# A layer kernel's value product: eight full products against seven products of halves, woven into the next unit's mixing

## The chip, the core and the metric

The kernel runs on one core of one Trainium2 chip. A core has a matrix engine (TensorE: PE for its products, PEld for its weight loads), a vector engine (VectorE: DVE), an activation engine (ScalarE: ACT), a general engine (GpSimd: POOL) and a queue that issues most transfers (SyncE: SP). Each engine takes its own instructions in the order in which the program emitted them and waits where an operand is not there yet. The metric is the device time of one execution in microseconds (us); the median of three runs of the kernel before is 1118.88 us (1118.39 to 1120.43).

## What is computed

One layer for x of 4 batches, 2048 tokens, 512 channels, all in f32: a linear recurrence, and after it the part that the change touches, a channel mix with a shift by one token:

```python
x_prev = concat([zeros, x[:, :-1]])              # x is the normalized, modulated h
xr = mu_r * x + (1 - mu_r) * x_prev
xk = mu_k * x + (1 - mu_k) * x_prev
r = sigmoid(xr @ W_r.T)                          # receptance
k_act = square(relu(xk @ W_k.T))                 # key
out = r * (k_act @ W_v.T)                        # value
...
x = x + gb * out                                 # gb: a gate per batch and channel
```

## The kernel before

The work is cut into 32 units of 256 tokens. Unit i is stretch i // 4 of batch i % 4; `at` below is i % 4. Two chains of units run at once, eight units apart: `Finish` (a unit's residual, normalization, key, receptance and value) and `Gates` (the projection for the recurrence of unit i + 8). The scan of the recurrence is a list of small DVE jobs handed out between by `take_share`, with the shares of a unit in SHARES. The order on every engine is the order of the calls, written out by hand.

A unit i from the fifth on does this on PE: the two "direct" products and the state products of unit i + 1 (L538, L493), woven between the seven products of the key (`seven`, L663, 28 matmuls of 128 columns, two PE instructions each); the seven products of the receptance (14 matmuls of 256 columns) with half of the projection of unit i + 8 (L244) between; then `mix` of unit i + 1, which begins with eight transposes (L600); the rest of the projection; and the value product (L760, eight matmuls of 512 columns). Units 0 to 3, 25 and 26 make the receptance with full products (L745), and units 0 to 3 the key too (L633).

`seven` makes seven products p1, p7, p6, p4, p5, p2, p3 in three PSUM tiles x, y, z. p1, p6, p5 and p3 use x one after the other and accumulate in it, p7 and p4 use z. After p1, p7, p6 and p3 ACT copies the tile out (L672, L675, L678, L690: the copies of the quarters c00, c11, c10, c01); after p4, p5 and p2 DVE adds it (L681, L684, L687). So p6 can't start before the copy of c00 is done, nor p4 before that of c11, p5 before that of c10, p3 before p5's addition. `emit` puts other jobs behind each product. Before `seven`, DVE makes four sums of quarters of the operand that varies (`sums_t` for the key, L779 to L782; `sums_s` for the receptance, L772 to L775).

`mix` of unit i + 1 (L585): after the transposes, eight times a pair of ACT (L606) and DVE (L609), the first four for the key, then POOL's edge column (L612), the four key sums and a small POOL copy behind them (L617), then `between` (both sigmoids of unit i on ACT, L737, and POOL's shift of the residual x of unit i + 2, L463), then four pairs for the receptance, a second edge and two small copies of the carry (L620). After it come, on DVE, `multiply` (L252: g, the projection times the row bc that came by DMA), on ACT `deliver` (L267: four instructions), the norm of a later unit's raw rows (L186, L192), and then the value product with its evictions on DVE (L763 times r, L764 plus x) and the store (L766).

The value weights carry the gate gb, so there is one set for each batch: the first four units scale w_v by gb (L978), turn it by 16 transposes (L992), copy it out (L996) and keep it in DRAM; a later unit fetches its set back, 1 MB a unit (L806). `Turn` does the same for D, scaled by ga, and that stays.

Of the kernel before, what the change touches and what calls it, by code (L numbers as in the profile page):

```python
# [21 lines left out]
P = 128  # L22
B, T, D, M = 4, 2048, 512, 64
KC = D // P
W = 256
# [22 lines left out]
def adaln_layer_kernel(ctx: ExitStack, tc: tile.TileContext, x, x_t, c_t, wmod, w_gate, w_b, b_gate, b_f, c_mat, d_mat,  # L48
# [18 lines left out]
    gb = const.tile([P, KC, B], F32, name="gb")  # L67
    d0 = const.tile([P, B, D], F32, name="d0")
# [6 lines left out]
    wvb = const.tile([P, B, KC, D], F32, name="wvb")  # L75
# [17 lines left out]
    d0c = const.tile([P, KC, B], F32, name="d0c")  # L93
# [344 lines left out]
    class Finish:  # L438
# [13 lines left out]
        def load(self):  # L452
            u = self.u
            if not hasattr(self, "x"):
                self.room()
                load_natural(u, self.x)
            if not hasattr(self, "h"):
                self.h = room_transposed(u)
                load_transposed(u, self.h)

        def shift(self, engine=nc.gpsimd):
            xt = self.x
            engine.tensor_tensor(xt, xt, d0[:, self.u.b, :].unsqueeze(1).broadcast_to([P, NT, D]), ALU.add)  # L463
# [121 lines left out]
        def mix(self, between):  # L585
            xn, b = self.xn, self.u.b
            mixed = self.mixed = p1.tile([P, 2, KC, W], F32, tag="mixed", name=f"mixed_{self.tag}")
            edge = p2.tile([P, 2, KC], F32, tag="edge", name=f"edge_{self.tag}")
# [6 lines left out]
            pts = []  # L595
            for g in range(KC // 2):
                pt = ps2.tile([P, 2, W], F32, tag="pt", name=f"pt_{self.tag}_{g}")
                for j in range(2):
                    for n in range(NT):
                        nc.tensor.transpose(pt[:, j, ts(n, P)], xn[:, n, ts(2 * g + j, P)], ident)  # L600
                pts.append(pt)

            for i in (1, 0):
                for k in (0, 2, 1, 3):
                    pt, m = pts[k // 2][:, k % 2, :], mixed[:, i, k, :]
                    nc.scalar.activation(  # L606
                        m, pt, AF.Identity, bias=mod[:, SB, k, b : b + 1], scale=now_f[:, b, i, k : k + 1]
                    )
                    nc.vector.scalar_tensor_tensor(  # L609
                        m[:, 1:], pt[:, : W - 1], prev_f[:, b, i, k : k + 1], m[:, 1:], ALU.mult, ALU.add  # L610
                    )
                nc.gpsimd.tensor_tensor(mixed[:, i, :, 0], mixed[:, i, :, 0], edge[:, i, :], ALU.add)  # L612
                if i == 1:
                    if self.fast:
                        self.key_sums()

                        nc.gpsimd.tensor_copy(edge[:, 1, 0:1], self.sums[:, 3, 1, W // 2 - 1 :])  # L617
                    between()
            for g, pt in enumerate(pts):
                nc.vector.tensor_copy(carry[:, b, 2 * g : 2 * g + 2], pt[:, :, W - 1])  # L620
# [88 lines left out]
        def key_sums(self):  # L709
            self.sums = self.half_of(dg[:, 3])  # L710
            sums_t(self.sums, self.token_quarters(1))
# [12 lines left out]
        def receptance_sums(self):  # L724
            self.r_sums = self.half_of(wvb[:, 3])
            sums_s(self.r_sums, list(zip(*self.token_quarters(0))))
# [8 lines left out]
        def sigmoids(self):  # L735
            for r in self.r:
                nc.scalar.activation(r, r, AF.Sigmoid)  # L737
# [12 lines left out]
        def value(self, between, parts=1):  # L750

            act, xt, u = self.act, self.x, self.u
            n_col = D // parts
            for n in range(NT):
                r = self.r[n]
                for h in range(parts):
                    at = ts(h, n_col)
                    pv = ps2.tile([P, D], F32, tag="pm", name=f"pv_{self.tag}_{n}_{h}")[:, :n_col]
                    for j, k in enumerate(range(KC) if parts == 1 else (2, 3, 0, 1)):
                        nc.tensor.matmul(  # L760
                            pv, act[:, k, ts(n, P)], wvb[:, self.at, k, at], start=(j == 0), stop=(j == KC - 1)
                        )
                    nc.vector.tensor_mul(r[:, at], pv, r[:, at])  # L763
                    nc.vector.tensor_add(r[:, at], r[:, at], xt[:, n, at])  # L764
                    queue = nc.scalar if h else nc.sync
                    queue.dma_start(out[u.b, u.t0 + n * P : u.t0 + (n + 1) * P, at], r[:, at])  # L766
                if n == 0:
                    between()
# [8 lines left out]
    def sums_t(t, b):  # L777
        (b00, b01), (b10, b11) = b
        nc.vector.tensor_sub(t[:, 0], b01, b00)  # L779
        nc.vector.tensor_sub(t[:, 1], b11, t[:, 0])  # L780
        nc.vector.tensor_sub(t[:, 2], b11, b01)
        nc.vector.tensor_sub(t[:, 3], b10, t[:, 1])  # L782

    def quarters_of(w, output_first=False):
# [4 lines left out]
    key_weights, receptance_weights = (  # L789
        room.rearrange("p k d -> p (k d)").rearrange("p (i k o) -> p i k o", i=4, k=2) for room in (dg[:, 2], wvb[:, 2])  # L790
    )

    kept = {
        name: [dram.tile([P, KC * D], F32, tag=f"{name}{b}", name=f"{name}{b}") for b in range(B)]
        for name in ("dg", "wv")
    }

    def keep_in_dram(name, b):
        src = dg if name == "dg" else wvb
        nc.sync.dma_start(kept[name][b], src[:, b].rearrange("p k d -> p (k d)"))  # L800

    def fetch(name, i):

        if 6 <= i < len(fin):
            dst = dg if name == "dg" else wvb
            nc.sync.dma_start(dst[:, i % 2].rearrange("p k d -> p (k d)"), kept[name][i % B])  # L806
# [56 lines left out]
    dn, wn = wr, wvb[:, 3]  # L863
    room = p2.tile([P, B, W], F32, tag="y", name="room").rearrange("p b w -> p (b w)")
    cn = room[:, :D].rearrange("p (k n) -> p k n", k=KC)
    d0row = room[:B, D:]

    ct, sig = d0c, off
# [156 lines left out]
    def shift_rows():  # L1025

        t = dram.tile([B, D], F32, tag="d0", name="d0_rows")
        nc.sync.dma_start(t, d0row)
        nc.sync.dma_start(d0, t.unsqueeze(0).broadcast_to([P, B, D]))
# [60 lines left out]
    weights_to(wn, w_v, nc.sync)  # L1090
# [16 lines left out]
    turn_v = [Turn(wvb[:, b], wn, gb, b, None, "v") for b in range(B)]  # L1107
# [17 lines left out]
    for e in range(KC):  # L1125
        nc.tensor.transpose(pr[:B, ts(e, P)], d0c[:, e, :], ident)
    nc.scalar.copy(d0row, pr[:B, :])
# [3 lines left out]
    keep_in_dram("dg", 0)  # L1131
# [17 lines left out]
    keep_in_dram("dg", 1)  # L1149
# [17 lines left out]
    turn_v[0].rows()  # L1167
# [40 lines left out]

    EIGHT = (25,26)
    SHARES = ((0,0,2,1.7,4.4, 0, 1.8), (5.4, 0.0, 1.8, 1.8, 3.6, 0.0, 1.8), (0.3, 0, 0.1, 0.1, 0.2, 0.03, 0.1))  # L1210
    for i, f in enumerate(fin):
        at = i % B
        ahead = fin[i + 1] if i + 1 < len(fin) else None
        if i < 4:
            if i == 3:
                take(100)
            fin[i + 2].load()
            gts[i + 10].load()
            f.key()
            if i == 0:  # L1220
# [22 lines left out]
            turn(turn_v[i])  # L1243
            keep_in_dram("wv", i)
            if i == 3:
                fetch("dg", i + 3)
# [13 lines left out]
            ahead.mix(fin[i + 2].shift)  # L1260
# [6 lines left out]
            if i < 3:  # L1267
                turn_v[i + 1].rows()
            f.value(lambda: take(3 if i == 0 else 4))
            if i < 2:  # L1270
                turn(turn_d[i + 2], turn_c[i + 2])
                keep_in_dram("dg", i + 2)
                gates(8 if i == 0 else 10)
        else:


            held = at == B - 2 and i > 4
# [6 lines left out]
            if not late:  # L1284
                load_finish()
            shares = [0] * 7
# [23 lines left out]
            def first_norm(j):  # L1310
                if j < len(gts):
                    gts[j].norm()

            def transfers(j):

                if j < len(gts):
                    gts[j].send()
                if j + 1 < len(gts):
                    gts[j + 1].load()
                fetch("wv", j - 7)  # L1320

            def spread():
                if 4 < i < len(gts) - 8:
                    gts[i + 8].spread()
# [5 lines left out]
            if not ahead:  # L1330
# [10 lines left out]
                f.squares(0)  # L1341
                f.emit(other[5:])
                finish = None
            elif late:
# [5 lines left out]
                f.emit(f.key_fast(), {1: [filler(d, 1), lambda: first_norm(i + 8)], 7: [filler(d, 1)],  # L1350
                                      6: [filler(d, 1)], 4: [filler(d, 1), f.receptance_sums],
                                      5: [filler(d, 1)], 2: [filler(d, 1)]})
                if i > 4:
                    transfers(i + 8)
                spread()
                fetch("dg", i + 3)
# [7 lines left out]
                          6: [filler(gate, 1), finish_norm], 4: [filler(gate, 1), lambda: f.squares(1)]}  # L1364
            else:
# [6 lines left out]
                                      6: [filler(d, 2), scans[1], acts[1], stats(0)],  # L1372
                                      4: [filler(d, 2), scans[2]], 5: [filler(d, 1), scans[3]],
                                      2: [stats(1, 0)], 3: [stats(1, 1), scans[4]]})
                fetch("dg", i + 3)
                spread()
# [3 lines left out]
                          5: [lambda: f.squares(1)]}  # L1380
# [5 lines left out]
            elif ahead:  # L1386
                f.emit(f.receptance_fast(), finish)

            def between():
                if not eight:  # L1390
                    f.sigmoids()
# [3 lines left out]
            if ahead:  # L1395
                ahead.mix(between)
            else:
                f.sigmoids()
            if i + 9 < len(gts):
                gts[i + 9].load_t()  # L1400
            fill(gate, len(gate))
# [3 lines left out]
            if not held:  # L1405
                first_norm(i + 9)
            f.value(scans[6], parts=1 if ahead else 2)
            if not held:
                transfers(i + 9)
# [46 lines left out]
```

## Time and profile before

| what | us |
|---|---|
| median of three runs | 1118.88 |
| span of the profiled execution | 1117.2 |
| PE busy | 1092.6 |
| DVE busy | 777.3 |
| ACT busy | 666.1 |
| POOL busy | 188.7 |
| one steady unit (value start to value start) | 32.1 |

PE is busy for all but about 25 us of the span, and these lie at the start and at the very end. The other engines are busy for two thirds of it or less. Matmuls overlap their neighbours in the records, so the time that one takes is read from start to start. A projection ("pg"), a direct product ("pd"), a key, receptance or value product ("px", "py", "pz" with the letter k or r, and "pv") can be told by the names of the tiles that they write.

### The profile page before, as it was taken

To read this page: it belongs to the slowest core of one execution; us is meant where nothing else is said; L and a number is where in the kernel's file an instruction comes from. 1 tells how busy PE (TensorE), PEld (TensorE's weight loads), DVE (VectorE), ACT (ScalarE), POOL (GpSimd) and SP (SyncE) were. 2 spreads that over 40 slices of the span, in tenths; PEclk is the share of its full clock that TensorE was granted. 3 is DMA by queue.
4 is the path that set the end of the run, shared out by engine and by line. 5 is a ranking of instruction groups with operands and counts; after the bars stand their busy time and mean duration, and the time that the engine had idled before them with its cause. 6 is when DMAs were issued, how large, how long until landed. Compare 5 with 4: busy or idle time off the path is not lost.

```text
span 1117.2 us, 14907 instructions
## 1 busy us (share of the span) xinstructions
PE 1092.6 (98%) x4772; PEld 738.4 (66%) x4772; DVE 777.3 (70%) x2158; ACT 666.1 (60%) x1380; POOL 188.7 (17%) x389
## 2 busy tenths in 40 slices
PE   7898999999999999999999999999999999999998
PEld 4566666657766666677666677766667665566666
DVE  5897777656877588766976577856887668764444
ACT  1655886647655777557655775647666474435443
POOL 1222201121112121111211112112121111111110
PEclk8879999999999999999999999999999999999999
DMA  9895395453447555565546756464445533443211
GB/s 312 309 175 139 94 157 159 108 170 100 124 137 191 127 168 175 165 133 172 111 156 204 166 166 161 142 142 130 164 169 182 150 119 132 142 151 132 95 57 38
DMA packets 133991, 168.32 MB, mean 151 GB/s; under 512 B 22292, under 2 KB 96788, under 8 KB 126104
## 3 DMA queue, kind: packets, MB, share of 16 engines
q1 hardware_dynamic: 130904, 166.03, 53.1%
q10 hardware_dynamic: 2688, 0.79, 0.3%
q0 software_dynamic: 320, 0.53, 0.3%
q8 instruction: 38, 0.62, 0.2%
q14 instruction: 41, 0.34, 0.1%
HBM read 137.90 MB, written 25.23 MB: 146 GB/s over the span
## 4 chain that ended last, share of the span: by engine, by line
PE 89%; DMA 5%; ACT 3%; DVE 2%; issue 1%; POOL 0%; SPq 0%; DVEq 0%; POOLq 0%; ACTq 0%
PE pv_c L760 18%; PE pd_c L538 16%; PE pxk_c L663 9%; PE pxr_c L663 8%; PE pg L244 6%; PE pzk_c L663 4%; PE pd_c L493 4%; PE pzr_c L663 4%; PE pd_c L470 3%; PE pr_c L745 2%; PE pg L234 2%; PE pt_c L600 2%; PE pyk_c L663 2%; PE pyr_c L663 2%; PE pk_c L633 2%; DMA xt<-in_x_t_dram 1%
## 5 line engine op out<-in xcount | busy, mean ns | idle before, releaser
L760 PE MATMUL pv_c<-wvb,act_c 128*128 128x512 f32 (+1 forms) x528 | 225.0, 579 | 0.0
L538 PE MATMUL pd_c<-dg,xt 128*128 128x512 f32 x432 | 206.2, 593 | 0.0
L609 DVE SCALAR_TENSOR_TENSOR mixed_c<-pt_c,prev_f,mixed_c 128x255 f32<-128x255 f32 x256 | 118.1, 481 | 77.5 <-ACT mixed_c L606 77.1
L760 PEld LDWEIGHTS pv_c<-wvb,act_c 128*128 128x128 f32 x528 | 99.5, 190 | 105.7 <-issue 100.2
L606 ACT ACTIVATE mixed_c<-pt_c,mod,now_f 128x256 f32<-128x256 f32 x256 | 130.2, 559 | 22.0 <-DVE mixed_c L609 16.2
L538 PEld LDWEIGHTS pd_c<-dg,xt 128*128 128x128 f32 x432 | 74.5, 191 | 55.9 <-issue 55.9
L244 PE MATMUL pg<-xt,wgb 128*128 128x256 f32 x320 | 85.4, 379 | 0.0
L478 DVE SCALAR_TENSOR_TENSOR x<-pd_c,rs,x 128x512 f32<-128x512 f32 x64 | 47.6, 745 | 52.0 <-PE pd_c L493 47.3
L557 ACT ACTIVATE xn_c<-x 128x512 f32<-128x512 f32 x44 | 27.7, 628 | 88.6 <-DVE x L478 84.1
L267 ACT ACTIVATE pre<-g,bias 64x256 f32<-64x256 f32 x56 | 41.6, 743 | 60.7 <-DVE g L252 51.4
L663 PEld LDWEIGHTS pxk_c<-dg 128*128 128x128 f32 x448 | 58.6, 191 | 26.4 <-issue 23.9
L463 POOL TENSOR_TENSOR x<-x,d 128x1024 f32<-128x1024 f32 x30 | 70.8, 2361 | 0.2 <-issue 0.2
L244 PEld LDWEIGHTS pg<-xt,wgb 128*128 128x128 f32 x320 | 59.2, 190 | 7.2
L580 ACT ACTIVATE xn_c<-x,mean_c,var_c 128x512 f32<-128x512 f32 x64 | 48.6, 808 | 21.8 <-POOL mean_c L576 21.8
L663 PE MATMUL pxk_c<-dg 128*128 128x128 f32 x448 | 59.2, 275 | 0.0
L493 PE MATMUL pd_c<-cg,y 128*128 128x512 f32 x112 | 56.3, 593 | 0.0
L663 PE MATMUL pxr_c<-wvb 128*128 128x256 f32 x208 | 53.4, 379 | 0.0
L612 POOL TENSOR_TENSOR mixed_c<-mixed_c,edge_c 128x4 f32<-128x4 f32 x64 | 12.9, 202 | 217.4 <-ACT mixed_c L606 216.9
L763 DVE TENSOR_TENSOR r_c<-pv_c,r_c 128x512 f32<-128x512 f32 (+1 forms) x66 | 43.9, 665 | 6.5 <-PE pv_c L760 6.5
L764 DVE TENSOR_TENSOR r_c<-r_c,x 128x512 f32<-128x512 f32 (+1 forms) x66 | 44.6, 676 | 2.3
L196 POOL TENSOR_SCALAR var<-var 128x2 f32<-128x2 f32 x26 | 10.5, 402 | 202.8 <-ACT xs L192 202.7
L252 DVE TENSOR_TENSOR g<-pg,bc 128x512 f32<-128x512 f32 x32 | 22.0, 688 | 32.0 <-DMA bc<-st 22.4
(261 smaller groups left out, 2140.2 us busy)
## 6 DMA issues: line engine op xcount, KB each, us to landing
dg<-dg SPq DMA_DIRECT2D x30, 1024.0 KB, 13.0
xt<-in_x_t_dram SPq DMA_DIRECT2D x116, 256.0 KB, 7.5
wvb<-wv SPq DMA_DIRECT2D x26, 1024.0 KB, 14.8
x<-in_x_dram SPq DMA_DIRECT2D x32, 512.0 KB, 15.0
out_dram<-r_c SPq DMA_DIRECT2D x62, 256.0 KB, 2.0
xs<-in_x_dram SPq DMA_DIRECT2D x54, 256.0 KB, 12.0
wvb<-in_wmod_dram SPq DMA_DIRECT2D x5, 1024.0 KB, 9.0
y<-pre SPq DMA_DIRECT2D x64, 64.0 KB, 2.0
```

Source lines behind the costliest of these rows:

```text
L244: nc.tensor.matmul(self.pg[:, i, :], wgb[:, u.b, k, ts(i, P)], self.xt[:, k, :], start=(k == 0), stop=(k == KC - 1))
L463: engine.tensor_tensor(xt, xt, d0[:, self.u.b, :].unsqueeze(1).broadcast_to([P, NT, D]), ALU.add)
L478: nc.vector.scalar_tensor_tensor(xt, pd, r, xt, ALU.mult, ALU.add)
L493: nc.tensor.matmul(pc, y_of[u.s][:, u.b, ts(n, P)], cg[:, u.b, :], start=start, stop=True)
L538: nc.tensor.matmul(pds[n], self.h[:, k, ts(n, P)], dg[:, self.at, k, :], start=(k == 0), stop=False)
L580: nc.scalar.activation(self.xn[:, n, :], self.x[:, n, :], AF.Identity, bias=self.mean[:, n : n + 1], scale=self.var[:, n : n + 1],)
L606: nc.scalar.activation(m, pt, AF.Identity, bias=mod[:, SB, k, b : b + 1], scale=now_f[:, b, i, k : k + 1])
L609: nc.vector.scalar_tensor_tensor(m[:, 1:], pt[:, : W - 1], prev_f[:, b, i, k : k + 1], m[:, 1:], ALU.mult, ALU.add)
L663: nc.tensor.matmul(to[:, j, :], left[:, k, ts(j, P)], right[:, k, :], start=start and j == k == 0, stop=(k == 1), skip_group_check=True,)
L760: nc.tensor.matmul(pv, act[:, k, ts(n, P)], wvb[:, self.at, k, at], start=(j == 0), stop=(j == KC - 1))
L763: nc.vector.tensor_mul(r[:, at], pv, r[:, at])
L764: nc.vector.tensor_add(r[:, at], r[:, at], xt[:, n, at])
```

## The change

The value product becomes a third use of `seven`: v in SBUF, in the room of xn, then r times v plus x. The value weights are w_v as it is (its transpose is laid out by the host), in one set that stays in SBUF, with four sums of its quarters made once. The gate gb is no longer in the weights: POOL multiplies it into the two halves of the receptance (`gate`), from a row that each unit loads by DMA (`load_row`). `mix` is cut into its pairs, and a new function puts the pairs of unit i + 1, the rest of the projection, the sigmoid, the gate, the shift and the results between the seven value products. `multiply` and `deliver` stay behind the whole. The norm of the raw rows moves from the end of a unit into the key products of the next, in two parts. The last unit has its own sequence. Units 25 and 26 keep the full receptance.

```diff
-    d0 = const.tile([P, B, D], F32, name="d0")
...
+        def load_row(self, which):
+            tag = ("d0", "gb")[which]
+            t = p2.tile([P, D], F32, tag=tag, name=f"{tag}_{self.u.tag}")
+            nc.sync.dma_start(t, col_rows[which : which + 1, self.u.b, :].broadcast_to([P, D]))
...
+        def gate(self, n):
+            nc.gpsimd.tensor_tensor(self.r[n], self.r[n], self.gate_row, ALU.mult)
...
-        def value(self, between, parts=1):
...
-                        nc.tensor.matmul(
-                            pv, act[:, k, ts(n, P)], wvb[:, self.at, k, at], start=(j == 0), stop=(j == KC - 1)
-                        )
-                    nc.vector.tensor_mul(r[:, at], pv, r[:, at])
-                    nc.vector.tensor_add(r[:, at], r[:, at], xt[:, n, at])
...
+        def value_sums(self):
+            self.v_sums = self.half_of(dg[:, 3] if self.fast else wvb[:, 0])
+            sums_s(self.v_sums, self.act_quarters())
+
+        def value_products(self):
+            v = self.v = p1.tile([P, NT, D], F32, tag="xn", name=f"v_{self.tag}")
+            return self.seven(
+                self.act_quarters(), self.v_sums, quarters_of(wv), value_weights,
+                [[v[:, n, ts(o, D // 2)] for o in range(2)] for n in range(NT)], "v",
+            )
+
+        def result(self, n, parts=1):
...
+                nc.vector.tensor_mul(r[:, at], self.v[:, n, at], r[:, at])
+                nc.vector.tensor_add(r[:, at], r[:, at], self.x[:, n, at])
...
+    def value_beside_mix(f, ahead, before=lambda: None, behind=lambda: None, fillers=(), between=lambda: None):
...
+        ahead.turn()
+        products = f.value_products()
+        ahead.mix_one(1, 0)
+        ahead.mix_one(1, 2)
+        f.emit(products, {
+            1: [lambda: filler(1), lambda: ahead.mix_one(1, 1)],
+            7: [lambda: ahead.mix_one(1, 3), lambda: ahead.mix_edge(1), lambda: sums(0)],
+            6: [lambda: filler(1), before],
+            4: [lambda: ahead.mix_one(0, 0)],
+            5: [lambda: filler(2), lambda: sums(1), behind, lambda: ahead.mix_one(0, 2), lambda: f.result(1)],
+            2: [lambda: filler(4), between, lambda: ahead.mix_one(0, 1)],
+            3: [lambda: ahead.mix_one(0, 3), lambda: ahead.mix_edge(0), ahead.keep_carry, lambda: f.result(0)],
+        })
...
+            if i == 0:
+                sums_t(value_weights, quarters_of(wv))
...
-            turn(turn_v[i])
-            keep_in_dram("wv", i)
+            f.value_sums()
...
-            ahead.mix(fin[i + 2].shift)
+            for n in range(NT):
+                f.gate(n)
...
-            f.value(lambda: take(3 if i == 0 else 4))
+            value_beside_mix(f, ahead, behind=fin[i + 2].shift, between=lambda: take(3 if i == 0 else 4))
             if i < 2:
                 turn(turn_d[i + 2], turn_c[i + 2])
...
-                fetch("wv", j - 7)
...
-                f.emit(f.key_fast(), {1: [filler(d, 1), lambda: first_norm(i + 8)], 7: [filler(d, 1)],
+                f.emit(f.key_fast(), {1: [filler(d, 1), lambda: first_norm(0), lambda: first_norm(1)], 7: [filler(d, 1)],
...
-                                      6: [filler(d, 2), scans[1], acts[1], stats(0)],
-                                      4: [filler(d, 2), scans[2]], 5: [filler(d, 1), scans[3]],
+                                      6: [filler(d, 2), scans[1], acts[1], lambda: first_norm(0), stats(0)],
+                                      4: [filler(d, 2), lambda: first_norm(1), scans[2]],
+                                      5: [filler(d, 1), scans[3]],
...
-                fetch("dg", i + 3)
-                spread()
+                transfers()
+                fetch(i + 3)
...
-                          5: [lambda: f.squares(1)]}
+                          5: [lambda: f.squares(1), f.value_sums]}
...
+                finish[5] += [lambda: f.sigmoid(1), lambda: f.gate(1)]
                 f.emit(f.receptance_fast(), finish)
+            spread()
+
+            def before():
                 if not eight:
-                    f.sigmoids()
+                    f.sigmoid(0)
+
+            def behind():
+                f.gate(0)
                 if i + 2 < len(fin):
                     fin[i + 2].shift()
 
-            if ahead:
-                ahead.mix(between)
...
-            fill(gate, len(gate))
+            value_beside_mix(f, ahead, before, behind, gate, scans[6])
             if i + 8 < len(gts):
                 gts[i + 8].multiply()
                 gts[i + 8].deliver()
-            if not held:
-                first_norm(i + 9)
-            f.value(scans[6], parts=1 if ahead else 2)
-            if not held:
-                transfers(i + 9)
```

## The prediction

> **What bounds the kernel now.** I read the busy shares and the clock row first, then who PE waited for, then the order in time around one unit.
>
> ```profile
> PE 1092.6 (98%) x4772; PEld 738.4 (66%) x4772; DVE 777.3 (70%) x2158; ACT 666.1 (60%) x1380; POOL 188.7 (17%) x389
> ...
> PEclk8879999999999999999999999999999999999999
> ```
>
> ```profile
> PE pxr_c L663 <- DVE r_c L684: 0.5, 1, 0.5
> ```
>
> The second is the whole list of PE's waits from 300 us to the end: one, of 0.5 us. So PE's work is the time, as long as ACT and DVE serve it in time; what the change takes from PE counts in full, and so does each new wait. PE's start times:
>
> ```profile
> 589.47 1.03 PE L663 MATMUL pxr_c<-wvb 128*128 128x256 f32 x4
> 590.34 1.03 PE L663 MATMUL pyr_c<-wr,mixed_c 128*128 128x256 f32 x4
> ...
> 594.73 7.03 PE L760 MATMUL pv_c<-wvb,act_c 128*128 128x512 f32 x16
> 601.60 1.88 PE L538 MATMUL pd_c<-dg,xt 128*128 128x512 f32 x4
> ```
>
> ```profile
> 196.58 1.91 PE L992 MATMUL turn_v<-ident,wvb 128*128 128x128 f32 x16
> 198.33 1.88 PE L745 MATMUL pr_c<-wr,mixed_c 128*128 128x512 f32 x4
> ```
>
> **What PE saves.** The value product takes 601.60 - 594.73 = 6.87 us a unit. One of the seven products of halves (four instructions of 256 columns) takes 590.34 - 589.47 = 0.865, seven 6.05. That is 0.82 x 32 = 26.2 us. Turning the weights takes 198.33 - 196.58 = 1.75, in four units 7.0. Together -33.2 us. That halves might not save is excluded: the receptance already does this shape at this pace.
>
> **Where the stall will be.** What the next unit's key needs first is the copy of c00 on ACT, and it stands behind `deliver`. Before, around the value end of unit 10:
>
> ```profile
> 472.78 0.69 DVE L252 TENSOR_TENSOR g<-pg,bc 128x512 f32<-128x512 f32 x1 [2.35 <-DMA bc<-st]
> ...
> 473.51 1.50 ACT L267 ACTIVATE pre<-g,bias 64x256 f32<-64x256 f32 x2 [3.72 <-DVE g L252]
> ...
> 475.02 1.50 ACT L267 ACTIVATE f<-g,bias 64x256 f32<-64x256 f32 x2
> ...
> 476.33 0.41 ACT L672 COPY act_c<-pxk_c 128x256 f32<-128x256 f32 x1
> ...
> 478.36 1.05 PE L663 MATMUL pxk_c<-dg 128*128 128x128 f32 x8
> ...
> 479.41 0.35 ACT L675 COPY act_c<-pzk_c 128x256 f32<-128x256 f32 x1
> ...
> 480.12 1.05 PE L663 MATMUL pzk_c<-dg,wk 128*128 128x128 f32 x8
> ```
>
> The chain is g, `deliver` (about 3.0), copy of c00, then p6 at 478.36; here the norm (2.65 us of ACT) lies before the copy of c11 and p4. The copies end 1.6 us before p6 and 0.4 before p4. With t = 0 at the start of the transposes (463.6), g ends at t = 9.8, held by a DMA; without this it could have been done at about 8 (unit 8: 407.8 - 399.4 = 8.4).
>
> After the change g stands behind everything that is put between the value products. I follow the queues with the durations of these rows, t = 0 at the transposes. PE: transposes 0.87, p1 ends 1.73, p7 3.03, p6 3.9, p4 5.2, p5 6.06, p2 7.8, p3 8.65 (four projection matmuls of 0.43 between). ACT: copies of c00, c11, c10 end at 2.25, 3.55, 4.45, each in time for the next product, so inside the value product PE doesn't wait. DVE: the four key pairs end at 4.6 (0.48 each, paced by ACT's 0.53 and the copies); then in a row two key sums 0.8, p4's addition 0.35, a pair 0.45, p5's addition 0.35, two sums 0.75, a pair 0.45, the result of one half 1.3 (0.7 + 0.6), p2's addition 0.35, two pairs 0.9, carry 0.2, the other result 1.3, g 0.6. That sums to 7.8: g ends at t = 12.4, plus the scan jobs put before it, which were 1.73 us (at = 0), 0.7 (at = 1), 1.06 (at = 2) and 0 in the trace. `deliver` and the copy add 3.45: c00 is out at 15.9 plus scan.
>
> PE comes to the next key's p6 at 8.65 + two direct matmuls 1.72 + p1 0.89 + two 1.72 + p7 0.89 + one 0.86 = 14.73; where the next unit is at = 3, with one instead of two behind p1, at 13.87. The wait in each:
>
> - into at = 0: 15.9 - 14.73 = 1.2
> - into at = 1: 1.73 of scan, and 0.35 because the sigmoid's table load (1.28 us) now comes before the pairs: 3.25
> - into at = 2: 0.7 of scan: 1.9
> - into at = 3: 15.9 + 1.06 - 13.87 = 3.1, and again at p4, because the norm still lies before c11: copy at 15.9 + 1.06 + 2.65 + 0.35 = 20.0 against p4 ready at 18.7: 1.25
>
> That is 10.7 in a round of four units, five rounds (a projection is there in units 4 to 23): +53.5 us. A stall doesn't use itself up: the next chain starts again from PE's transposes.
>
> **The first units.** In units 0 and 1 the turn of D follows the value product and needs the two PSUM tiles that `mix` reads; their last reader is the carry copy. In unit 0 DVE is busy until 127.7 (other units' statistics), then come now the sums (2.8 for the weights, partly in an idle 2.25, and 1.55), the pairs from about 130 on and 3.75 us of scan before the last pairs: carry at about 141.6, where PE started the turn at 132.3. With the 2.6 that PE saves this is a stall of 11.9. In unit 1 the carry comes at t = 13.65 (4.9 of scan), the value product ends at 6.95: 6.7, less the 1.3 of DMA wait there: 5.4. Together +17.3.
>
> **Covered parts.** DVE's four value sums (1.55) lie under the end of the receptance, where it waited 0.3 to 0.4 for PE; ACT's four more copies are 1.5 a unit. If that cover is gone the heaviest unit shows it:
>
> ```profile
> 402.00:434.00 32.00, 32.00 (x145) 22.23 (x144) 27.31 (x75) 21.27 (x46) 6.17 (x11) 1.00 0.43 145
> ```
>
> DVE 27.3 of 32, and 2.9 more (seven of 0.42) makes 30.2 of the 31.2 that would be left: no reserve for in-order waits, up to 1 us in each of six such units, which the 3.25 us stall there covers already. Off ACT and DMA go 8.1 + 10.2 us of copies and scalings and 30 MB of weights; 64 loads of 256 KB on SP come in, ahead of their use by a unit: nothing on the path. `send` and `spread` of a unit move to one key and receptance: by 10.0 us and 8.4 us to landing bc comes at about t = 12, against g's start at 11.8: nothing to 1 us, and I take nothing. The last unit ends with a copy more: 0.5. POOL's gate is half of L463's 2361 ns, 1.2 each; L617's copy, the shift and the second edge are queued behind it, and the next receptance sums wait for that edge, but PE needs these only after p4 of the key: nothing.
>
> **What POOL may do to DVE.**
>
> ```profile
> L196 POOL TENSOR_SCALAR var<-var x26: 191/192/1394, 51.0 to 865.4; 128x2 f32<-128x2 f32 x26
> ```
>
> The same two-column instruction takes 0.19 or, beside DVE's products of two SBUF tiles (479.6: 0.88), up to 1.39 us; the shift today runs only beside pairs that read PSUM and is 2.36 in all 30. Now gate and shift meet the results, which read two SBUF tiles. No row shows DVE waiting for POOL; the bounds are 0 and 1.0 + 2.4 = 3.4 us a unit (up to 68 us), and I take 0, since DVE's rows beside POOL are all of normal length. [...]
>
> **Sum.** Against the execution shown: 1117.2 - 33.2 + 53.5 + 17.3 + 0.5 = 1155.3. The median lies 1.7 above that span: **1157**.
>
> The clock is 1.00 in every later row and fell to 0.50 once, behind 3.2 us without PE work at 42 us. [...]
>
> **Rivals.**
> - *PE stays gapless.* For: ACT is 60% busy, all copies inside the value product are in time. Against: it needs g by t = 11, with 4.6 + 7.8 us of DVE work before it. Time 1118.9 - 33.2 + 0.5 = 1086; with half of the stalls off (g put earlier than I read it) up to 1121.
> - *POOL holds DVE.* One mechanism on the slow side: gate and shift beside the results, 3.4 us a unit in 20 units, from the point where POOL's gate overlaps the first result: 1157 + 68 = 1225. For: the stretched POOL rows. Against: no DVE row is stretched.
> - *Even.* Stalls of 33 us, about half of mine: 1119, by chance only.
>
> **Chances.** A change is told from none at about 0.2%. Stalls from ACT's order, 1121 to 1200: 0.52; POOL on top, above 1200: 0.22; gapless or nearly, below 1116: 0.22; even: 0.04. Faster 0.22, same 0.04, slower 0.74. The likeliest's own range is 1125 to 1195. The range has to hold 8 in 10: 1098 (five sixths of the 71 us of stalls gone) to 1240 (the lock in full).
>
> **What would show it.** PE waits at L663 for ACT's copies of the key's c00 and, in at = 3 units, c11; `deliver` starts 12 to 14 us after the transposes; PE waits at L992 in units 0 and 1 for the carry. Value products of 6.05 us. A stretched L764 beside POOL would prove the second rival; a PE without waits would prove me wrong, and then the error is in DVE's queue ahead of g.

## The result, and the profile after

The changed kernel takes 1275.26 us (1269.19 to 1276.12) against 1119.66 us for the one before on the same chip: ratio 1.137, interval 1.135 to 1.140. The prediction had the direction and the place, and 118 us too little. The profiled execution has a span of 1274.4 us. First its busy row and its clock row:

```profile
PE 1119.0 (88%) x5076; PEld 832.0 (65%) x5076; DVE 955.2 (75%) x2384; ACT 689.9 (54%) x1476; POOL 298.9 (23%) x453
...
PEclk9889899999898999999988998898999899999999
```

PE has less to compute than before and is busy longer, 1119.0 us against 1092.6; it idles 155.4 us against 24.6. The clock row, all nines before but for the first slices, has eights through the middle. Whom PE waited for (total us, times, longest):

```profile
PE pxk_c L689 <- ACT act_c L698: 102.5, 20, 6.9
PE turn_d L1022 <- DVE carry L633: 11.8, 2, 6.7
PE pxv_c L689 <- ACT v_c L698: 6.2, 4, 4.9
```

The first row is the stall that was predicted: ACT's copy of the key's c00, once in each of the 20 units that follow a projection. Only it is 102.5 us, where 47.3 were predicted for these copies. The order in time around the value product of unit 9 tells why (the transposes started at 479.74, t = 0):

```profile
487.36 1.27 POOL L475 TENSOR_TENSOR r_c<-r_c,gb 128x512 f32<-128x512 f32 x1
487.40 1.78 DVE L795 TENSOR_TENSOR r_c<-v_c,r_c 128x512 f32<-128x512 f32 x1
...
488.59 2.81 POOL L472 TENSOR_TENSOR x<-x,d 128x1024 f32<-128x1024 f32 x1
...
489.21 2.73 DVE L796 TENSOR_TENSOR r_c<-r_c,x 128x512 f32<-128x512 f32 x1
...
493.80 0.68 DVE L795 TENSOR_TENSOR r_c<-v_c,r_c 128x512 f32<-128x512 f32 x1
494.51 0.69 DVE L796 TENSOR_TENSOR r_c<-r_c,x 128x512 f32<-128x512 f32 x1
495.12 0.68 DVE L251 TENSOR_TENSOR g<-pg,bc 128x512 f32<-128x512 f32 x1
...
495.84 1.48 ACT L266 ACTIVATE pre<-g,bias 64x256 f32<-64x256 f32 x2 [6.42 <-DVE g L251]
...
497.33 1.46 ACT L266 ACTIVATE f<-g,bias 64x256 f32<-64x256 f32 x2
...
498.81 0.37 ACT L698 COPY act_c<-pxk_c 128x256 f32<-128x256 f32 x1
...
499.24 2.08 PE L689 MATMUL pxk_c<-dg 128*128 128x128 f32 x8 [4.61 <-ACT act_c L698]
```

The same two result instructions stand there twice. Alone they take 0.68 and 0.69 us. Beside POOL's gate and shift they end some 0.55 us behind POOL's instruction, as if they had begun only about then: the first takes 1.78 and ends at 489.18, behind a gate of 1.27 that ends at 488.63; the second takes 2.73 and ends at 491.94, behind a shift of 2.81 that ends at 491.40. That is 3.1 us (491.94 - 487.40 = 4.54, less 1.4) ahead of g, which ends at t = 16.1 instead of the 13.1 of my queue (12.4 and 0.7 of scan). The rest of the chain is as drawn: g, delivery of 3.0, copy, p6. PE would have been at p6 at t = 14.9 (499.24 - 4.61 - 479.74; predicted 14.73).

The last row shows a second thing. Eight matmuls of 128 columns take 2.08 us there, twice the 1.05 of the prediction's row of this product. In 17 of the 20 units the group behind this wait is as slow. The granted clock (last column but two) in stretches of 2 us around it:

```profile
496.00:498.00 2.00, 0.00 (x0) 1.00 0.80 196
498.00:500.00 2.00, 0.76 (x3) 0.73 1.00 321
500.00:502.00 2.00, 2.00 (x9) 0.50 0.97 319
502.00:504.00 2.00, 2.00 (x9) 0.91 0.73 205
```

While PE is idle the row still says 1.00; once work comes back it runs at 0.50 until about 502. Over the whole execution the stretched groups are (count, busy us, mean ns):

```profile
L796 DVE TENSOR_TENSOR r_c<-r_c,x 128x512 f32<-128x512 f32 (+1 forms) x65 | 93.9, 1445 | 2.2
...
L472 POOL TENSOR_TENSOR x<-x,d 128x1024 f32<-128x1024 f32 x30 | 82.9, 2762 | 0.0
...
L795 DVE TENSOR_TENSOR r_c<-v_c,r_c 128x512 f32<-128x512 f32 (+1 forms) x65 | 68.6, 1056 | 0.6 <-DVE v_c L710 0.5
```

Before, the same three were:

```profile
L764 DVE TENSOR_TENSOR r_c<-r_c,x 128x512 f32<-128x512 f32 (+1 forms) x66 | 44.6, 676 | 2.3
...
L463 POOL TENSOR_TENSOR x<-x,d 128x1024 f32<-128x1024 f32 x30 | 70.8, 2361 | 0.2 <-issue 0.2
...
L763 DVE TENSOR_TENSOR r_c<-pv_c,r_c 128x512 f32<-128x512 f32 (+1 forms) x66 | 43.9, 665 | 6.5 <-PE pv_c L760 6.5
```

### The profile page after: what moved, and what is told of

It is laid out like the page before. It is cut to its first block, busy times and chain, and to the rows that moved or that the text cites. A ratio compares the mean times of both kernels' runs of the same rounds, so it can differ in the third digit from the quotient of the medians.

```text
span 1274.4 us, 16098 instructions
## 1 busy us (share of the span) xinstructions
PE 1119.0 (88%) x5076; PEld 832.0 (65%) x5076; DVE 955.2 (75%) x2384; ACT 689.9 (54%) x1476; POOL 298.9 (23%) x453
## 4 chain that ended last, share of the span: by engine, by line
PE 52%; DVE 28%; ACT 15%; issue 3%; DMA 1%; POOL 1%; DVEq 0%; POOLq 0%; ACTq 0%; SPq 0%
PE pd_c L550 9%; PE pxk_c L689 7%; DVE r_c L796 6%; PE pxr_c L689 5%; DVE r_c L795 4%; DVE mixed_c L619 4%; PE pzr_c L689 3%; PE pg L243 3%; PE pd_c L482 3%; PE pxv_c L689 3%; PE pg L233 3%; PE pd_c L505 2%; ACT mixed_c L618 2%; ACT f L266 2%; ACT pre L266 2%
## 5 line engine op out<-in xcount | busy, mean ns | idle before, releaser
L550 PE MATMUL pd_c<-dg,xt 128*128 128x512 f32 x432 | 229.5, 651 | 0.0
L689 PE MATMUL pxk_c<-dg 128*128 128x128 f32 x448 | 76.8, 326 | 102.5 <-ACT act_c L698 102.5
L689 PEld LDWEIGHTS pxk_c<-dg 128*128 128x128 f32 x448 | 71.0, 233 | 136.2 <-ACT act_c L698 119.1
L475 POOL TENSOR_TENSOR r_c<-r_c,gb 128x512 f32<-128x512 f32 x64 | 88.7, 1388 | 149.0 <-ACT r_c L763 113.9
L796 DVE TENSOR_TENSOR r_c<-r_c,x 128x512 f32<-128x512 f32 (+1 forms) x65 | 93.9, 1445 | 2.2
L689 PE MATMUL pxv_c<-wvb,dg 128*128 128x256 f32 x336 | 87.2, 382 | 1.0 <-ACT v_c L698 1.0
L472 POOL TENSOR_TENSOR x<-x,d 128x1024 f32<-128x1024 f32 x30 | 82.9, 2762 | 0.0
L707 DVE TENSOR_TENSOR act_c<-act_c,pzk_c 128x256 f32<-128x256 f32 x28 | 11.7, 419 | 86.5 <-PE pzk_c L689 64.3
L689 PEld LDWEIGHTS pxv_c<-wvb,dg 128*128 128x128 f32 x336 | 63.1, 190 | 12.3 <-DVE v_c L710 2.2
L795 DVE TENSOR_TENSOR r_c<-v_c,r_c 128x512 f32<-128x512 f32 (+1 forms) x65 | 68.6, 1056 | 0.6 <-DVE v_c L710 0.5
L569 ACT ACTIVATE xn_c<-x 128x512 f32<-128x512 f32 x44 | 27.6, 627 | 73.0 <-DVE x L490 68.2
L592 ACT ACTIVATE xn_c<-x,mean_c,var_c 128x512 f32<-128x512 f32 x64 | 48.6, 807 | 27.6 <-POOL mean_c L588 27.6
```

Of the source, the lines that this page charges most:

```text
L472: engine.tensor_tensor(xt, xt, self.shift_row.unsqueeze(1).broadcast_to([P, NT, D]), ALU.add)
L475: nc.gpsimd.tensor_tensor(self.r[n], self.r[n], self.gate_row, ALU.mult)
L550: nc.tensor.matmul(pds[n], self.h[:, k, ts(n, P)], dg[:, self.at, k, :], start=(k == 0), stop=False)
L592: nc.scalar.activation(self.xn[:, n, :], self.x[:, n, :], AF.Identity, bias=self.mean[:, n : n + 1], scale=self.var[:, n : n + 1],)
L689: nc.tensor.matmul(to[:, j, :], left[:, k, ts(j, P)], right[:, k, :], start=start and j == k == 0, stop=(k == 1), skip_group_check=True,)
L795: nc.vector.tensor_mul(r[:, at], self.v[:, n, at], r[:, at])
```

## The experiments

Three things had to be told apart: what stands ahead of the copy of c00 (order), what POOL takes from DVE (holding), and what the gaps do to PE's clock. A fourth possibility was that DVE is simply full.

**1. POOL's gate and shift left out**

```
     def behind():
-        f.gate(0)
-        if i + 2 < len(fin):
-            fin[i + 2].shift()
+        pass
...
-    finish[5] += [lambda: f.sigmoid(1), lambda: f.gate(1)]
+    finish[5] += [lambda: f.sigmoid(1)]
```

> The changed kernel without POOL's gate (units 4 to 31) and without POOL's shift of x for units 6 to 31; these parts of the computation are left out. [...] Rival (DVE is simply full with the added sums, POOL is incidental): the results keep their length, waits fall by under 20 us, the time stays above 1240.

Four of the 56 gates stay (one half in units 25 and 26, both in the last unit). Measured: 1174.61 us, ratio 1.052 (1.049 to 1.055), span 1172.4. The results are back, and PE's waits fall:

```profile
L796 DVE TENSOR_TENSOR r_c<-r_c,x 128x512 f32<-128x512 f32 (+1 forms) x65 | 46.5, 715 | 2.2
...
L795 DVE TENSOR_TENSOR r_c<-v_c,r_c 128x512 f32<-128x512 f32 (+1 forms) x65 | 43.9, 676 | 0.2
```

```profile
PE pxk_c L689 <- ACT act_c L698: 39.9, 20, 3.8
PE turn_d L1022 <- DVE carry L633: 11.7, 2, 6.7
```

POOL's pieces are worth 102.0 us of span. 69.2 of these are idle time of PE (155.4 - 86.2), 32.8 are PE's own busy time (1119.0 - 1086.2). The waits for the copy of c00 alone give 62.6 of the first (102.5 - 39.9), 3.1 a unit, as the rows of unit 9 had it. In the round from 391 us on the waits are 0.84, 2.36, 1.49 and 2.61 us; my queues had 1.2, 3.25, 1.9 and 3.1. So the order of the change costs what I had worked out, a little less, and the holding by POOL is the term that I had set to 0. My theory (POOL holds DVE, and the copy of c00 waits behind g) had these waits at 50 to 70 us and the time at 1155 to 1195. The waits fell further, but that PE's clock would stay up behind what is left of them had been an assumption, and the run shows otherwise: behind five of the 20, of 2.2 to 2.6 us, the group of matmuls was slow again (1.72 to 2.08 us instead of 1.16).

**2. g ahead of the results, with and without POOL's pieces**

```
-    5: [..., behind, lambda: ahead.mix_one(0, 2), lambda: f.result(1)],
-    2: [lambda: filler(4), between, lambda: ahead.mix_one(0, 1)],
-    3: [lambda: ahead.mix_one(0, 3), ..., ahead.keep_carry, lambda: f.result(0)],
+    5: [..., behind, lambda: ahead.mix_one(0, 2), mul],
+    2: [lambda: filler(4), lambda: ahead.mix_one(0, 1)],
+    3: [dlv, lambda: ahead.mix_one(0, 3), ..., ahead.keep_carry, lambda: f.result(1), between, lambda: f.result(0)],
```

> The changed kernel with g put on DVE directly behind the mixing pair (0,2), its delivery on ACT directly behind the copy of the value's last product, and both results behind the carry. POOL's work stays. Theory (order): g at about 9 us after the transposes, c00's copy out at about 13.3, before PE comes to p6 at 14.7: the waits for it fall from 102.5 to under 25; what POOL holds of DVE now falls behind g, and costs only where DVE has no reserve: 1110 to 1160. Rival (the lock on DVE costs wherever it falls): waits move to other operands of PE, the time stays above 1210.

> Both edits together: no gate and no shift on POOL (left out of the computation), and g ahead of the results. Theory: PE has no gap left outside the first units, 1117 - 33 + 17 = about 1102 (1095 to 1115). Rival (DVE full): waits for DVE's sums or additions appear, above 1140. If the value product of halves doesn't save 0.8 us a unit, above 1115 without any waits.

Measured: 1195.40 us with POOL (1.071, 1.068 to 1.074) and 1185.62 without (1.062, 1.059 to 1.065). Both miss their theory; the second lies where its rival, a full DVE, had it. The waits for c00 did go, to 1.7 and 2.0 us, but another took their place in both; in the one without POOL's pieces:

```profile
PE pxk_c L689 <- DVE act_c L710: 55.4, 16, 6.6
```

This is DVE's addition of the key's fifth product. In time (the same kernel) one sees what made it late:

```profile
463.72 1.48 ACT L266 ACTIVATE f<-g,bias 64x256 f32<-64x256 f32 x2
465.21 0.56 ACT L618 ACTIVATE mixed_c<-pt_c,mod,now_f 128x256 f32<-128x256 f32 x1
...
465.81 0.48 DVE L619 SCALAR_TENSOR_TENSOR mixed_c<-pt_c,prev_f,mixed_c 128x255 f32<-128x255 f32 x1 [3.68 <-ACT mixed_c L618]
```

I had put the delivery ahead of ACT's half of the last mixing pair, and DVE, in order, stood 3.68 us for it with results, sums and scan queued behind: here DVE is late because it waits, not because it is full (experiment 7 settles it). The time that PE had lost for c00 had also been time in which DVE caught up. That waits of this kind don't add up is the lesson: without POOL's pieces g first is slower (1186) than without the move (1175).

**3. POOL's pieces kept and moved**

```
+    def early():                      # called ahead of the value products
+        fin[i + 2].shift()
+        f.gate(1)
     def before():
         f.sigmoid(0)
+        f.gate(0)
     def behind():
-        f.gate(0)
...
+        pass
```

> The changed kernel, complete, with POOL's three pieces moved: the shift and gate of half 1 directly behind the transposes, beside the mixing pairs that read PSUM, the gate of half 0 directly behind its sigmoid, ahead of the copy that closes the key sums. Theory (POOL holds only DVE instructions with two SBUF inputs): the results are back at 0.7 us, the shift at about 2.4, the time within 20 us of the kernel without POOL's pieces: 1155 to 1205. Rival (POOL's volume costs wherever it lies): the pairs of the mixing get longer by as much as the results had been, time above 1240.

Measured: 1203.05 us (1.078, 1.074 to 1.081), with all of the computation. The results are back at 676 and 715 ns and the shift at 2407, so 67 to 72 us of the loss (by ratio or by time) went by moving three instructions on an engine that is 23% busy. Not all did; 28 us more than in experiment 1 are left, where at most 20 were expected. The shift waited for nothing and ran ahead of the transposes, beside the scan (a scan product of 0.23 us, L395, took up to 2.27 there), and the gate of half 1 met the last value sum, which takes 0.42 elsewhere:

```profile
458.08 1.53 POOL L475 TENSOR_TENSOR r_c<-r_c,gb 128x512 f32<-128x512 f32 x1 [3.26 <-ACT r_c L763]
...
458.39 1.50 DVE L805 TENSOR_TENSOR dg<-act_c,dg 128x256 f32<-128x256 f32 x1
```

PE now waits 13.5 us for DVE's additions of the receptance, against 0.8 in experiment 1.

**4. The gate alone left out**

The edit is that of experiment 1 with the shift left in.

> The changed kernel without POOL's gate in units 4 to 31 (left out of the computation), the shift kept. Theory: each POOL piece costs what it holds DVE ahead of g. Without the gate of half 0 DVE gets back about 1.1 us ahead of g; the shift now meets the result of half 1 about 1.2 us earlier and holds it as long as before. Waits for c00 fall from 102.5 by 20 times 1.1 to about 80, less 1 us for the value sums: 1215 to 1245. Rival (the gate is the whole of it): near 1175, as without both. Rival (the shift is the whole): above 1265.

Measured: 1242.03 us (1.113, 1.111 to 1.115). PE's largest wait:

```profile
PE pxk_c L689 <- ACT act_c L698: 83.4, 20, 6.0
```

Each piece costs about what it holds: the gate 19.1 us of these waits (102.5 - 83.4), and with the shift out too another 43.5 go (83.4 - 39.9). That is 1.0 and 2.2 us a unit; the rows of unit 9 show 1.1 and 2.0 held.

**5. The delivery behind the copy of c00**

```
-    gts[i + 8].deliver()              # behind multiply, ahead of the next key
+    f.emit(f.key_fast(), {1: [filler(d, 2), rest], ...    # rest: gts[i + 7].deliver()
```

> The changed kernel with one step moved: ACT's delivery of g stands behind the next key's copy of c00 instead of ahead of it; DVE and POOL as they were. Theory: the waits for the copy of c00 (102.5 us) fall below 15, since nothing late stands ahead of it; but PE's wait had also given DVE its time, and as in the kernels with g ahead of the results new waits for DVE's additions of the key (L710) of 40 to 80 us appear: 1160 to 1215. Rival (order of ACT alone is the whole loss): no new waits, 1105 to 1140. Rival (the copy of c00 was late for another reason than deliver): waits for it stay, above 1240.

Measured: 1240.37 us (1.111, 1.109 to 1.114). The waits for c00's copy are gone, but neither theory had what came: the next copy, of c11, now stands behind the late g, the delivery and (in a round's last unit) the norm.

```profile
PE pzk_c L689 <- ACT act_c L701: 68.7, 20, 8.0
PE pxk_c L689 <- DVE act_c L710: 15.1, 11, 2.9
```

ACT's order was the place where the loss showed. Its cause was g's lateness on DVE, and that went with the copy that was put behind it.

**6. More work for PE in the gap**

```
     def p7():
+        if name == "k" and 4 < self.u.i < 25:
+            for _ in range(4):
+                product(z, s[:, 2], t[:, 2])
         nc.scalar.copy(c11, product(z, s[:, 2], t[:, 2]))
```

> The changed kernel with more work for PE: in units 5 to 24 the key's second product is computed five times into the same PSUM tile, the last one kept (3.6 us of added matmuls a unit, 71 us in all, output complete). They lie where PE waits 3.9 to 6.9 us for the copy of c00; the wait that is left is 0.4 to 3.3 us. Theory (behind a gap of that length PE runs at half clock for 2 to 4 us, and this is on the path, since the next chain starts from PE): the matmul behind the wait (8 of 128 columns) falls from 2.08 to about 1.16 us, and the kernel gets faster although it computes more: by 20 times 1 to 2 us, 1235 to 1255. Rival (those matmuls are slow for another reason, traffic on PSUM or SBUF): they stay at 2.08, the time is the same within 5 us or longer, 1270 to 1290.

Measured: 1247.68 us (1.116, 1.112 to 1.120), 27.6 us faster than the changed kernel with 71 us more of matmuls. The waits for c00 fall by what was put in (102.5 to 31.4). In 15 of the 20 units the group behind the wait takes 1.16 us, in five still 1.42 to 2.08. In unit 5:

```profile
299.69 1.02 PE L505 MATMUL pd_c<-cg,y 128*128 128x512 f32 x2
302.63 1.16 PE L689 MATMUL pxk_c<-dg 128*128 128x128 f32 x8 [1.92 <-ACT act_c L698]
303.62 1.88 PE L550 MATMUL pd_c<-dg,xt 128*128 128x512 f32 x4
```

Since work and wait cancel, the 24 to 28 us (by ratio or by time) are the clock's. Its record agrees: PE was busy at half clock for 118.6 us in the changed kernel and for 63.7 here. Work at half clock takes about twice as long (2.08 us for the group above, against 1.16), so by an estimate half of the difference, 27 us, is what it cost.

**7. The order mended throughout**

```
     5: [lambda: filler(2), lambda: sums(1), ..., mix_one(0, 2), mix_one(0, 1), mix_one(0, 3), mix_edge(0), keep_carry],
     2: [lambda: filler(4), mul, lambda: f.result(1)],
     3: [dlv, between, lambda: f.result(0)],             # dlv: pre only; f behind the next key's c00
...
-    SHARES = ((0,0,2,1.7,4.4, 0, 1.8), (5.4, ...
+    SHARES = ((0,0,2,1.7,4.4, 1.8, 1.8), (3.6, ...
...
```

> The changed kernel, complete, with its order mended: all mixing pairs and the carry ahead of g, g ahead of both results, ACT's delivery in two halves (the two rows of pre behind the copy of the value's last product, the two of f behind the next key's copy of c00), POOL's shift behind the gate of half 1 (beside the pairs that read PSUM), the gate of half 0 directly behind its sigmoid, the norm of the coming unit one product earlier, and two scan jobs' worth (1.8 us) moved from the heaviest unit of a round (at = 1) into the one before. Theory: g ends about 10 us after the transposes, c00's copy at 12 to 13 against PE's 14.7, DVE has 31 us of work at most against PE's 31.3: PE's waits for c00 under 10 us in all, for DVE's additions under 20, the time 1085 to 1115, below the kernel before. Rival (DVE is full, order can't help): waits for DVE's additions of 40 us or more stay, time above 1120.

Measured: 1130.48 us (1.012, 1.011 to 1.014): 140 to 145 us less than the changed kernel (by ratio or by time) with all of the computation in place, and still 14 more than the kernel before on the same chip. The waits came out as the theory had them, none for c00 and 18.0 us for DVE's additions, where the rival (DVE is full) asked for 40 or more; the time did not: it lies above the 1115 of the theory. PE's largest waits now (of 56.9 us of idle time):

```profile
PE pxv_c L691 <- DVE v_c L712: 8.9, 7, 1.6
PE pxr_c L691 <- DVE r_c L712: 5.9, 6, 2.2
```

**8. The gate on DVE, then DVE's queue shortened, then both by unit**

```
-                finish[5] += [lambda: f.sigmoid(1), lambda: f.gate(1)]
+                finish[5] += [lambda: f.sigmoid(1)]
...
+                if self.fast:                                               # in result, ahead of each
+                    nc.vector.tensor_mul(r[:, at], r[:, at], self.gate_row[:, at])
```

> The kernel with the mended order, its gate taken from POOL to DVE (one product of two SBUF tiles ahead of each result, an estimated 0.69 us like L795), and POOL's shift back behind the copy that closes the key sums, where DVE now has only pairs, the carry, an addition from PSUM and g. Theory (POOL holds DVE's two-SBUF instructions): the value sum beside the gate is back from 1.50 to 0.43 us, the key sum from 1.54 to 0.43, the waits in the last units without projection (1.8 us each) and those of 0.8 to 3.0 us in the units that follow a round's last one go; DVE's own work grows by 1.4 us a unit and loses 2.2 of holding: 1100 to 1120. Rival (DVE's volume is what counts): with 1.4 us more the heavy units (27.5 of 31.3) wait for DVE, 1125 to 1140.

> The kernel with the gate on DVE, and DVE's queue ahead of the key's fifth product made shorter: the gate of half 1 in a gap where DVE waits for ACT between the first mixing pairs (0.7 us), the scan's jobs that stood ahead of that product's addition put behind it or a unit earlier (1.7 to 2 us in the two heavy units), one half of the late unit's norm one product later, in the last unit the gates ahead of the value's additions. Theory (PE's remaining waits are DVE work put ahead of the additions that PE needs): the two heavy units fall from 32.8 and 33.2 us to 31.5 to 31.8, the waits of 0.7, 0.6 and 0.8 us in the two others go, together some 4.8 us in five rounds: 1136 - 24 = 1112 (1104 to 1122). Rival (DVE's volume, 29 of 31.3 us, decides, wherever it is put): the waits move to the receptance's additions, 1128 to 1140.

> The two former kernels put together unit by unit: where DVE has 27.5 us and more of its own to do (the value products of a round's first two units, up to unit 23) the gate stays on POOL as in the kernel with the mended order, with the shift behind the gate of half 1; in all other units it is on DVE as in the kernel with the gate on DVE, with its places for gate and norm; the scan's shares as in the first of the two but for 1.8 us moved back. Theory (holding by POOL is paid where DVE has reserve, DVE's own work where it has none): 31.3 and 31.6 us in the heavy units, 31.6 and 32.0 in the light ones, 28.0 to 28.3 in the last: 1126 - 11 = 1115 (1109 to 1121), the same as before or a little faster. Rival (the two don't combine, since a late DVE of one unit is handed to the next): 1124 to 1135.

Measured: 1136.39 us (1.018, 1.017 to 1.020), 1126.15 (1.008, 1.005 to 1.010) and 1125.47 (1.007, 1.006 to 1.009). All three lie above their theory's range, the first and the third where the rival had them. One heavy unit (the second of a round) and one of the last units, which have no projection, first with the gate on POOL (experiment 7), then with it on DVE. The columns are start:end, us, busy us of PE, PEld, DVE, ACT and POOL, then the clock, the share of DMA and GB/s:

```profile
399.19:430.46 31.27, 31.27 (x157) 24.58 (x156) 27.56 (x76) 21.61 (x49) 9.21 (x14) 1.00 0.71 154
...
1033.98:1064.19 30.21, 28.45 (x142) 21.21 (x140) 17.64 (x37) 15.30 (x38) 7.21 (x10) 1.00 0.21 70
```

```profile
400.62:433.44 32.82, 31.52 (x158) 24.64 (x157) 28.99 (x78) 21.62 (x49) 6.29 (x11) 1.00 0.67 170
...
1042.86:1070.86 28.00, 28.00 (x141) 21.34 (x140) 17.34 (x39) 15.43 (x38) 4.55 (x8) 1.00 0.24 75
```

Each mechanism shows in its own units. Where DVE has reserve, taking the gate off POOL (and putting the shift back) removes 2.2 us (30.21 to 28.00, below the 28.62 of before). Where it has none, 1.4 us more of DVE work costs 1.5 (31.27 to 32.82): DVE is busy with one break of 0.24 us from the fifth microsecond to the receptance, and PE waits for its addition to the key. Moving scan jobs behind that addition moved the wait to the receptance's addition, as the rival had it (15.8 us there in the second kernel), and choosing by unit gained nothing more. None of the versions here beats the kernel before.

## Why the prediction was wrong, point by point

- **PE's saving: right.** Seven products take 6.04 us (480.61 to 488.38 less 1.73 for four projection matmuls), predicted 6.05; a unit of the last kernel in which PE never waits (722.95 to 754.20) takes 31.25 us, and 32.08 - 0.82 is 31.26. But it is 26 us in all, less than any of the losses.
- **The place of the stall: right, and its size without POOL nearly right**: 39.9 us measured (experiment 1) against 47.3 for the copies of c00 (53.5 less five times 1.25); for c11 1.5 against 6.25.
- **"No row shows DVE waiting for POOL; the bounds are 0 and 1.0 + 2.4 = 3.4 us a unit (up to 68 us), and I take 0": this is the step that failed.** The waits for c00 put it at 3.1 us a unit, 62.6 in all (102.5 - 39.9), and PE's whole idle time at 69.2: the upper end. The reason that I gave, DVE's rows of normal length, was no evidence: before, POOL's only long instruction ran beside pairs that read PSUM, so the meeting that the change brings had never taken place in that trace. The one row that did show a meeting, a POOL instruction stretched from 0.19 to 1.39 us, showed it from POOL's side. In the changed kernel results are held (up to 2.73 us, 0.68 alone) and sums (up to 1.51, 0.42 alone), pairs, carry and g, which read PSUM, are not (0.49, 0.15 and 0.69 us at most; last section).
- **The clock: in no term of the sum, and it cost about 47 us; the second step that failed.** PE was busy at half clock for 24.5 us before and for 118.6 in the changed kernel, and half of the difference is loss (an estimate, as in experiment 6). With the holding, gaps reach 3.9 to 6.9 us, and I had gone by the gaps that I predicted (up to 3.25 us) and not by those of the rival that I gave 22%. But not that alone: without POOL's pieces (experiment 1, gaps up to 3.8 us) 59.3 us are still at half clock, a loss of 17. That gaps of the predicted size leave the clock alone was an assumption of mine; behind 10 of 22 waits of 1.9 to 2.9 us PE was slow again (last section). The trace before had spoken against it: its clock fell not once but three times, the last time at 63.82 us, behind a wait of 1.83 us. The columns are start:end, us, busy us of PE, clock, share of DMA and GB/s:

```profile
60.41:63.82 3.41, 1.57 (x12) 1.00 0.73 41
63.82:67.23 3.41, 3.41 (x13) 0.50 0.63 207
```

  The holding lengthens the gaps (the longest is 6.9 us, against 3.8 without POOL's pieces), and the clock makes PE pay for them again. That is why the result lies beyond 1240, the end that was to hold "the lock in full". No run shows a lock as such; what the runs show in its place is single instructions held, 3.1 us a unit in the waits for c00.
- **The first units: half right.** The turn of D waits for the carry 11.8 us in two units; 17.3 was predicted. With the carry ahead of results and scan it is 3.2 (experiment 2) and 0.2 (experiment 7).
- **The last units: wrong.** I gave the last one 0.5. From its transposes to the end (1238.52 on) the time grows from 31.15 to 35.9 us, though the two value products there should save 1.6. Three waits for value and receptance sums make up 2.8 of it. And in the units ahead of it that have no projection (1058.74 to 1238.52) PE idles 7.4 us where it had no idle time before and my sum none.
- **The sum.** 1155.3 was forecast, 1274.4 came. Of the 119.1 between them 59.5 are idle time (155.4 against 95.9) and 59.6 PE's busy time (1119.0 against 1059.4), most of it the clock's 47. Without POOL's pieces the span is 1172.4: idle time is 9.7 less than I had (86.2 against 95.9), PE's busy time 26.8 more (1086.2 against 1059.4), 17 by half clock and about 5 because the first group behind each wait for c00 lasts 1.16 us instead of its 0.89 of pace. The rest of the 26.8 stays open.

## What to carry to other kernels

Before moving work to an idle engine, ask what that engine will run beside, not how busy it is: three POOL instructions of 5 us a unit cost 102 us here, some 30 of them through PE's clock, and a trace in which two things never meet says nothing about their meeting. When a bound is open at both ends, look for the row that shows the meeting from the other side, and carry the upper end through to what it triggers (here gaps long enough to slow PE). And where an engine waits, its wait may be the only time in which another catches up: move the last cause, not the place where it shows.

## What the runs showed of the hardware

- POOL and DVE held each other here, and only some of DVE's instructions were held. A result, 0.68 us alone, took 1.78 and 2.73 beside POOL, and POOL's gate took 1.39 in the mean, 1.27 with nothing to meet. Not only results and sums were held: a product of one SBUF tile and a constant (L319, experiment 3) took 0.19 us at the start and up to 1.94 beside the shift. But around a shift in the kernel with the gate on DVE (in order of time) the rows that read PSUM kept their length (a pair 0.48 us, g 0.69):

```profile
440.70 0.87 DVE L621 SCALAR_TENSOR_TENSOR mixed_c<-pt_c,prev_f,mixed_c 128x255 f32<-128x255 f32 x2
...
441.06 2.37 POOL L474 TENSOR_TENSOR x<-x,d 128x1024 f32<-128x1024 f32 x1
...
441.81 0.48 DVE L621 SCALAR_TENSOR_TENSOR mixed_c<-pt_c,prev_f,mixed_c 128x255 f32<-128x255 f32 x1 [0.24 <-ACT mixed_c L620]
...
442.67 0.69 DVE L251 TENSOR_TENSOR g<-pg,bc 128x512 f32<-128x512 f32 x1
```

- The clock fell behind shorter gaps than I had thought. PE's 80 waits for the copy of c00 in four kernels (the changed one and experiments 1, 4 and 6), by the length of the wait, and how often the group behind it took over 1.3 us instead of 1.16:

```
wait in us   under 1.9   1.9-2.9   2.9-3.7   3.7-4.3   over 4.3
waits               16        22         8         6         28
slow behind it       0        10         1         2         28
```

  In the record of the granted clock, in all thirteen traces, the clock changes only at points that lie whole multiples of 3.413 us apart, so the record divides into windows of that length. From 230 us on, the clock fell behind 98 windows at full clock, in which PE was idle for 1.9 us or more, and behind none of the 3370 others, in which it was idle for 2.0 us or less; in the changed kernel alone it fell behind 22, with 2.12 us of idle time or more, and behind none of 251 others, with 1.93 or less. So what a fall went with in these traces was not the length of a wait but how much of it fell into one window. Two waits of 2.61 us in experiment 1, the first inside one window, the second cut in two (columns as above):

```profile
504.97:508.38 3.41, 0.80 (x4) 1.00 0.54 181
508.38:511.79 3.41, 3.41 (x12) 0.50 0.45 107
778.03:781.45 3.42, 1.74 (x10) 1.00 0.34 125
781.45:784.86 3.41, 2.02 (x10) 1.00 0.47 125
```

- Adding 71 us of useless matmuls made the kernel 24 to 28 us faster (experiment 6).
